# Row tiles in one self attention, activation tables named ahead of use, and the last attention pass kept in PSUM banks

## The chip, the cores and the metric

The kernel runs on one core of one Trainium2 chip. The metric is the device time of one execution in microseconds (us), the median of several runs. One further execution was recorded by the hardware profiler; every duration of a single instruction comes from that one.

## The reference, cut to what matters

Two layers of a Perceiver-like block act on x (128 latents of 256 numbers) with a context of 12544 rows of 192 numbers. All is fp32.

```python
x = x + xattn0(layernorm(x), ctx)   # 16 heads of 16; softmax(q k^T / 4) v over 12544 keys, then relu(o W1 + b1) W2 + b2
x = x + attn0(layernorm(x))         # causal, 16 heads of 16, over the 128 latents, projection
x = x + ffn0(layernorm(x))          # 8 experts 256 -> 1024 -> 256, tanh-gelu, two best experts by a softmax router
x = x + xattn1(layernorm(x), ctx)   # 16 heads of 64; o Wo + bo
x = x + attn1(layernorm(x))         # softmax(x x^T / 16); probabilities under 0.01 are taken out, the others renormalised;
                                    # attended + 0.01 * (sum of those taken out) * (row sums of W)
x = x + ffn1(layernorm(x))          # 8 experts 256 -> 512 -> 256, silu(x G) * (x U) D, two best experts
```

The experts are computed densely: all eight for every latent, weighted by the router (zero for six of them).

## The kernel before, in words

The stages run one after the other, and the names in the trace carry their prefix: x_ in the cross attentions, ln1 to ln5 for the layer norms, k for key tiles made ahead, a_ in the self attentions, f_ in the experts.

**Engines.** TensorE (PE) multiplies into PSUM, eight banks of 128 x 512 fp32. VectorE (DVE), ScalarE (ACT) and GpSimd (POOL) copy, add and exponentiate. SyncE (SP) issues nearly all transfers, in order. Within `tc.manual_schedule()` every engine executes its instructions in the order in which the code writes them; elsewhere a scheduler chooses the order. Before the change, the end of x1 (from the load of Wo), a1 and f1 stand outside it.

**Buffers.** A ring of 28 slots of 128 x 1024 fp32 in SBUF holds score tiles, keys and weights (`slot`, `slot_weight`); a transfer into a slot waits until its last reader is done. In the second half PSUM is split: "s", two tiles of two banks, for scores (`ps_s`, `ps_wide`), and "w", four single banks (`ps_w`, `ps_t`, `ps_mm`). The context is read anew in thirteen superblocks of 1024 rows (the last has 256): `load_context` brings lo (128 rows of features, 512 KB) and hi (64 rows in two halves, 2 x 128 KB).

**x0, to 460 us.** Two octets of eight heads; scores on 32-row tiles of the array (L428: `x_qz`, a copy of q in which the head beside it is zeroed, against `x_kT`); each range of superblocks keeps its own maximum; shift (L506), exponential (L517), attend (L530). Then the ranges are combined (L675 to L703): the negative maxima's least, `fall` = the exponential of the difference, `accs` times `fall`, a sum over the ranges, the division; then W1, W2 and the residual (L706 to L725).

**Key steps.** From there to x1, PE has gaps. `first_keys` (L639 to L660) makes the keys of x1's first pass in 39 steps: for each superblock the 64-row tiles (`tiled`, L209) and two products over 128 rows (`whole`, L212). `fill(n)` makes n steps at the place where it stands. The copies out of the two banks (ACT, L655) are issued when the next superblock is begun. x1's first pass calls fill(2) or fill(1) per period until all are made.

**a0, 481 to 523 us** (L734 to L801). q, k and v are projected; `block_diagonal` (L160) multiplies q with a head mask into a tile of 8 x 128 columns for each eight heads; one matmul per head against the 128 rows of kT gives the scores (L766, a_s); mask, maximum, 16 exponentials (L773), transposition of p in groups of four (a_pT), attend with a column of ones (L785, a_av), division, transposition (a_oT), projection, residual, key steps.

**f0, 523 to 584 us** (L804 to L880). `up` (L824, f_h), bias, gelu (L834), `down` (L841, f_py), each expert's `up` ahead of the former one's `down`. The router (L256 to L300) is a softmax and twice a maximum.

**x1, 584 to 1524 us** (L883 to L1173). Eight passes j of one pair of heads (64 numbers each), thirteen periods s each; a period t makes keys, scores (L958), a copy with the running maximum (ACT L975, DVE L982 of the score tiles, two of 128 x 1024 per period, one for the last superblock), values (L227, L234), and, LAG = 14 periods later, the attend (L1043). At a pass's end the maximum is folded (DVE L1005), transposed (x_mt), negated, spread over the partitions by PE (x_mb) and copied by ACT (x_spread, L1017). The next pass's periods then shift the saved scores by it (`shifted`, L1024: POOL, but DVE in the last pass), exponentiate (L1032), attend; sums of p go by DVE and POOL (L1066, L1071), in the last pass by DVE into one tile (L1062); DVE adds each period's o (L1081). A denominator is the sums against ones (L1089). After the last scores (t = NP = 104) fourteen periods are left that make values and attend: the tail. Then Wo, row bo (L126), residual.

**a1, 1524 to 1541 us** (L1178 to L1222): row sums of W (a_pc, L1182, copied by ACT, L1184), scores, exponential (L1193), a row of small DVE operations, attend, x5. **f1, 1541 to 1588 us** (L1225 to L1261): for each expert gating and up (L1249), silu (L1253), product (f_fuse, L1255), down (L1258), weighted sum.

An ACT function that lies in another table set than the one before is preceded by an ACT_TABLE_LOAD, which the compiler places directly ahead of it: it stands in the trace under the line of that function.

## Time and profile before

| | us |
|---|---|
| median of three runs | 1596.47 |
| the three | 1592.82, 1597.17, 1596.47 |
| the profiled execution: its own time | 1592.66 |
| its span | 1590.9 |

| stage | us from the span's start |
|---|---|
| x0 | 0 to 460 |
| combine, W1, W2, ln1 | 460 to 481 |
| a0 | 481 to 523 |
| f0 | 523 to 584 |
| x1 with its tail (from 1447) | 584 to 1524 |
| a1 | 1524 to 1541 |
| f1, output | 1541 to 1591 |

A timeline line gives start, duration, engine, line, operation, out<-in, sizes, number, and in brackets how long the engine stood idle before it and what released it. Consecutive instructions of a kind are put together. In a line of a stage's busy times, "PEclk" is the mean clock that was granted to TensorE, 1.00 being full.

### The profile page before, as it was taken

To read this page: it belongs to the slowest core of one execution; us is meant where nothing else is said; L and a number is where in the kernel's file an instruction comes from. 1 tells how busy PE (TensorE), PEld (TensorE's weight loads), DVE (VectorE), ACT (ScalarE), POOL (GpSimd) and SP (SyncE) were. 2 spreads that over 40 slices of the span, in tenths; PEclk is the share of its full clock that TensorE was granted. 3 is DMA by queue.
4 is the path that set the end of the run, shared out by engine and by line. 5 is a ranking of instruction groups with operands and counts; after the bars stand their busy time and mean duration, and the time that the engine had idled before them with its cause. 6 is when DMAs were issued, how large, how long until landed. Compare 5 with 4: busy or idle time off the path is not lost.

```text
span 1590.9 us, 39751 instructions
## 1 busy us (share of the span) xinstructions
PE 1507.9 (95%) x17130; PEld 1156.8 (73%) x17130; DVE 1169.4 (74%) x1238; ACT 996.3 (63%) x1221; POOL 851.1 (54%) x559
## 2 busy tenths in 40 slices
PE   7999989999789998999999999999999999999978
PEld 4566666666545877877778787787787777777868
DVE  4798978999863327677777777777777777778952
ACT  5898979889853225665655665565665655655531
POOL 0588877888820000863863864864764764761000
PEclk9999999999997999999999999999999999999979
DMA  3211112111193661322222222232232222225930
GB/s 104 61 41 42 46 42 61 41 42 46 47 270 129 238 167 25 98 84 83 83 80 86 81 81 86 80 93 74 87 94 80 87 81 86 81 81 153 306 135 4
DMA packets 68737, 146.62 MB, mean 92 GB/s; under 512 B 8905, under 2 KB 27089, under 8 KB 68562
## 3 DMA queue, kind: packets, MB, share of 16 engines
q1 hardware_dynamic: 68258, 143.30, 30.0%
q8 instruction: 135, 2.21, 0.6%
q10 hardware_dynamic: 304, 0.79, 0.2%
q14 instruction: 40, 0.33, 0.1%
HBM read 143.92 MB, written 0.13 MB: 91 GB/s over the span
## 4 chain that ended last, share of the span: by engine, by line
PE 62%; DVE 6%; ACT 2%; POOL 1%; DMA 1%; issue 1%; SPq 0%; DVEq 0%; ACTq 0%
PE x_s L958 11%; PE x_v L234 10%; PE x_o L1043 10%; PE x_k L212 9%; PE x_v L227 5%; PE x_k L209 4%; PE f_h L1249 2%; PE f_h L824 2%; PE k L212 2%; PE f_py L841 2%; DVE x_part L1066 1%; POOL x_p L506 1%; PE k L209 1%; DVE x_folded L1005 1%; PE f_py L1258 1%
## 5 line engine op out<-in xcount | busy, mean ns | idle before, releaser
L1024 POOL TENSOR_TENSOR x_p<-x_p,x_spread 128x1024 f32<-128x1024 f32 (+1 forms) x175 | 402.6, 2324 | 165.1 <-ACT x_spread L1017 164.9
L506 POOL TENSOR_TENSOR x_p<-x_p,x_spread 128x512 f32<-128x512 f32 (+1 forms) x184 | 325.6, 1820 | 121.0 <-ACT x_spread L494 61.1
L1066 DVE TENSOR_REDUCE x_part<-x_p 128x256 f32<-128x1024 f32 (+1 forms) x175 | 329.4, 1923 | 1.6 <-ACT x_p L1032 1.6
L975 ACT COPY x_p<-x_s 128x1024 f32<-128x1024 f32 (+1 forms) x200 | 198.0, 996 | 177.7 <-DVE x_mx L982 97.9
L982 DVE TENSOR_TENSOR x_mx<-x_s,x_mx 128x1024 f32<-128x1024 f32 (+1 forms) x161 | 193.4, 1201 | 127.1 <-PE x_s L958 118.7
L1071 POOL TENSOR_TENSOR x_sums<-x_sums,x_part 128x256 f32<-128x256 f32 x161 | 118.7, 738 | 303.4 <-DVE x_part L1066 303.1
L441 ACT COPY x_p<-x_s 128x1024 f32<-128x1024 f32 x196 | 193.4, 1016 | 48.5 <-PE x_s L428 33.2
L234 PEld LDWEIGHTS x_v<-ywv_lo,x_ctx_lo 128*128 128x128 f32 x1568 | 189.3, 192 | 38.3 <-issue 36.8
L1032 ACT ACTIVATE x_p<-x_p 128x1024 f32<-128x1024 f32 (+1 forms) x200 | 197.8, 1037 | 1.4 <-DVE x_p L1024 1.3
L517 ACT ACTIVATE x_p<-x_p 128x1024 f32<-128x1024 f32 x196 | 196.3, 1062 | 0.2 <-DVE x_p L506 0.2
L1043 PE MATMUL x_o<-x_p,x_v 128*64 128x128 f32 x3136 | 193.6, 276 | 0.4
L234 PE MATMUL x_v<-ywv_lo,x_ctx_lo 128*128 128x128 f32 x1568 | 193.1, 276 | 0.0
L447 DVE TENSOR_TENSOR x_mx<-x_s,x_mx 128x1024 f32<-128x1024 f32 x140 | 168.2, 1221 | 32.1 <-PE x_s L428 17.2
L1043 PEld LDWEIGHTS x_o<-x_p,x_v 128*64 128x64 f32 x3136 | 169.6, 137 | 12.3 <-issue 1.5
L958 PE MATMUL x_s<-x_qT,x_kT 64*128 64x128 f32 x2744 | 177.7, 279 | 0.0
L212 PE MATMUL x_k<-x_ctx_lo,ywk_lo 128*128 128x512 f32 (+1 forms) x364 | 171.6, 594 | 0.0
L958 PEld LDWEIGHTS x_s<-x_qT,x_kT 64*128 64x128 f32 x2744 | 160.2, 188 | 15.6 <-issue 15.4
L943 ACT COPY x_v<-x_v 128x512 f32<-128x512 f32 (+1 forms) x208 | 116.2, 563 | 79.3 <-PE x_v L234 78.8
L227 PEld LDWEIGHTS x_v<-ywv_hi,x_ctx_hi 64*128 64x128 f32 x1568 | 106.8, 188 | 48.4 <-issue 25.1
L428 PE MATMUL x_s<-x_qz,x_kT 32*128 32x256 f32 x1568 | 117.6, 401 | 17.7 <-ACT x_p L441 16.6
L530 PE MATMUL x_o<-x_p,x_v 128*32 128x128 f32 x3136 | 111.7, 276 | 10.0 <-ACT x_p L517 8.5
L530 PEld LDWEIGHTS x_o<-x_p,x_v 128*32 128x32 f32 x3136 | 81.9, 109 | 53.9 <-ACT x_p L517 18.9
(257 smaller groups left out, 1761.1 us busy)
## 6 DMA issues: line engine op xcount, KB each, us to landing
x_ctx_lo<-in_ctxT_dram SPq DMA_DIRECT2D x119, 512.0 KB, 4.0
x_ctx_hi<-in_ctxT_dram SPq DMA_DIRECT2D x238, 128.0 KB, 3.8
f_w<-in_L_ffn_W_dram SPq DMA_DIRECT2D x32, 512.0 KB, 4.9
k_lo<-in_ctxT_dram SPq DMA_DIRECT2D x12, 512.0 KB, 10.0
f_gating<-n_kernel_gating_EDF_dram SPq DMA_DIRECT2D x8, 512.0 KB, 6.9
f_up<-L_ffn_kernel_up_EDF_dram SPq DMA_DIRECT2D x8, 512.0 KB, 7.5
f_wd<-ffn_kernel_down_EFD_dram SPq DMA_DIRECT2D x8, 512.0 KB, 7.3
k_hi<-in_ctxT_dram SPq DMA_DIRECT2D x24, 128.0 KB, 7.9
```

The lines of the kernel that those rows point to most:

```text
L212: nc.tensor.matmul(ps[r][:, :h], wk[0][:, js], lo[:, r * h : (r + 1) * h], start=False, stop=True)
L234: nc.tensor.matmul(ps[r][:, kc * P : (kc + 1) * P], lo[:, r * h + kc * P : r * h + (kc + 1) * P], wv[0][:, js], start=False, stop=True, sk ...
L441: nc.scalar.copy(ps[t][k], st[k].rearrange("p a n -> p (a n)"))
L506: engine.tensor_tensor(v, v, by[:, banks].unsqueeze(2).to_broadcast([P, n, 2, 256]), ALU.add)
L517: nc.scalar.activation(ps[t][k], ps[t][k], AF.Exp)
L530: nc.tensor.matmul(os[b][32 * i : 32 * i + 32, u * P : (u + 1) * P], v[:, 2 * g + c, 17 * (2 * i + u) : 17 * (2 * i + u) + 32], p[i // 2][ ...
L958: nc.tensor.matmul(st[:, u, c * P : (c + 1) * P], kTs[t][rs, ks], qT[rs, j, :], start=True, stop=True)
L975: nc.scalar.copy(scores_kept(ps[t][i], sts[i].shape[2] // P), sts[i])
L1024: engine.tensor_tensor(v, v, spreads[j].unsqueeze(2).to_broadcast([P, 2, n, P]), ALU.add)
L1032: nc.scalar.activation(v, v, AF.Exp)
L1043: nc.tensor.matmul(o[us, 0:P], vs[t][:, c0 + c, us], p[:, n0 : n0 + P], start=(c0 + c == 0), stop=(c0 + c == total - 1), skip_group_check= ...
L1066: nc.vector.tensor_reduce(part, v, AX.X, ALU.add)
```

## The change

- `table(func, name)` is a one-column ACTIVATE whose result nobody reads: it makes the table set load where it stands. Exp after each layer norm's std; Sqrt ahead of ln1 to ln5; Gelu in f0's router; Silu in f1.
- x0's two octets are combined each by itself (`octet`), the first one inside x0, after the last shift.
- Key banks are copied right after each `whole`, and the steps are spread anew: 7 instead of 11 in the combine, 15 instead of 13 in a0 with what follows up to x2, 26 instead of 28 in all before x1.
- a0's scores: q is kept in two copies (heads of one parity each), and each of 16 matmuls uses a 32-row tile of the array; scores and p lie in another order of heads.
- x1's last pass: when the last scores are read, their two double banks become `sums` (DVE adds p there) and `both` (PE accumulates o over all periods in one bank; the other takes the projection by Wo and the row sums of W). The shift of the first tile of a period stays on DVE and reads the spread in PSUM, that of the second goes to POOL. Wo is loaded at t = NP+1, seven of the projection's eight matmuls stand at t = NP+3. The contexts of t = NP+2, +5, +8, +11 go to ring slots.
- a1 and f1 are put in a written order; all of f1's weights are issued there, after the last context; expert e+1's gating and up stand ahead of e's down.

The diff, cut to its core:

```diff
@@ -126,6 +126,11 @@
+    def table(func, name):
+        scratch = small.tile([P, 1], F32, tag="table", name=name)
+        nc.scalar.activation(scratch, eps, func)
@@ -133,6 +138,7 @@
+        table(AF.Exp, name + "_table")
@@ -546,6 +550,24 @@
+            def octet(j, out):
+                bs = slice(j * nr, (j + 1) * nr)
+                allneg = small.tile([P, 8], F32, tag="allneg", name=f"x0_allneg{j}", bufs=1)
+                nc.vector.tensor_reduce(allneg, negmax[:, bs].rearrange("p b h -> p h b"), AX.X, ALU.min)
+                fall = small.tile([P, nr, 8], F32, tag="fall", name=f"x0_fall{j}", bufs=1)
+                nc.vector.tensor_tensor(
+                    fall, allneg.unsqueeze(1).to_broadcast([P, nr, 8]), negmax[:, bs], ALU.subtract
+                )
+                nc.scalar.activation(fall, fall, AF.Exp)
+                nc.vector.tensor_tensor(
+                    accs[:, bs], accs[:, bs], fall.unsqueeze(3).to_broadcast([P, nr, 8, 17]), ALU.mult
+                )
+                nc.vector.tensor_reduce(
+                    out.rearrange("p h d -> p (h d)"), accs[:, bs].rearrange("p b h d -> p (h d) b"),
+                    AX.X, ALU.add,
                 )
@@ -606,6 +628,8 @@
+                    if o == len(groups) - 1:
+                        octet(0, acc[0])
@@ -637,25 +661,16 @@
-                    out = None
...
-                        if out:
-                            out()
...
-                        whole(0)
-                        yield
-                        whole(1)
-                        def out(s=s, h=h, pk=pk):
-                            for r in range(2):
-                                nc.scalar.copy(firstk[s][:, r * h : (r + 1) * h], pk[r][:, :h])
-                        yield
-                    out()
+                        for r in range(2):
+                            whole(r)
+                            nc.scalar.copy(firstk[s][:, r * h : (r + 1) * h], pk[r][:, :h])
+                            yield
@@ -667,39 +682,22 @@
...
+                om, o = misc[:, :D], misc[:, D : 2 * D]
+                acc.append(misc[:, 512 : 512 + 8 * 17].rearrange("p (h d) -> p h d", d=17))
+                octet(1, acc[1])
+                table(AF.Sqrt, "ln1_table0")
...
+                    nc.vector.reciprocal(rden, acc[j][:, :, 16])
...
+                        acc[j].rearrange("p (u i) d -> p u i d", u=2)[:, :, :, 0:16],
...
+                fill(3)
@@ -722,7 +720,7 @@
-                fill(3)
+                fill(2)
@@ -737,7 +735,8 @@
-            qbd = work.tile([P, NH, P], F32, tag="qbd", name="a0_qbd")
+            qz = work.tile([P, 2, 2, P], F32, tag="qz", name="a0_qz")
@@ -749,7 +748,8 @@
-                    block_diagonal(work, qT, j, qbd)
+                    for u in range(2):
+                        nc.vector.tensor_scalar(qz[:, j, u, :], qT, parity[:, u : u + 1], None, ALU.mult)
@@ -759,21 +759,34 @@
+            heads = [[8 * g + 2 * (2 * k + i) + u for i in range(2) for g in range(2) for u in range(2)] for k in range(2)]
+            st = [ps_wide(f"a0_s{k}").rearrange("p a (b n) -> p a b n", n=P) for k in range(2)]
+            for g in range(2):
+                for u in range(2):
+                    for i in range(4):
+                        rs = slice(32 * i, 32 * i + 32)
+                        nc.tensor.matmul(
+                            st[i // 2][:, i % 2, 2 * g + u, :], qz[rs, g, u, :], kT[rs, g, :], start=True, stop=True
+                        )
...
+            fill(1)
+            for k in range(2):
+                sm = work.tile([P, 8, P], F32, tag="sm", name=f"a0_sm{k}", bufs=2)
+                nc.vector.tensor_tensor(
+                    sm, st[k].rearrange("p a b n -> p (a b) n"), causal.unsqueeze(1).to_broadcast([P, 8, P]), ALU.add
+                )
+                nmax = small.tile([P, 8], F32, tag="a_nmax", name=f"a0_nmax{k}")
...
+                p = work.tile([P, 8, P], F32, tag="ap", name=f"a0_p{k}", bufs=2)
...
+                if k:
+                    table(AF.Sqrt, "ln2_table0")
+                fill(1)
...
+            fill(2)
@@ -842,7 +856,7 @@
-        best = router(pl[:, :NE], "f0")
+        best = router(pl[:, :NE], "f0", AF.Gelu_apprx_tanh)
@@ -853,6 +867,8 @@
+                if e + 2 == NE:
+                    table(AF.Sqrt, "ln3_table0")
@@ -914,7 +930,9 @@
-            ctxs[t] = load_context(work, f"x1_ctx{t}", (t + 1) % NS, 2)
+            place = slot if t >= NP and (t - NP) % 3 == 2 else None
+            ctxs[t] = load_context(work, f"x1_ctx{t}", (t + 1) % NS, 2, place=place)
@@ -1011,19 +1029,25 @@
+            if j == PASSES - 1:
+                final["sums"] = ps_s("x1_sums")
+                final["both"] = ps_s("x1_both")
...
+            if j == PASSES - 1:
+                final["spread"] = pb
...
-            for p, (c0, n) in zip(ps[t], tiles_of(s)):
+            for i, (p, (c0, n)) in enumerate(zip(ps[t], tiles_of(s))):
...
-                engine = nc.gpsimd if j < PASSES - 1 else nc.vector
-                engine.tensor_tensor(
-                    v, v, spreads[j].unsqueeze(2).to_broadcast([P, 2, n, P]), ALU.add
-                )
+                engine, by = nc.gpsimd, spreads[j]
+                if j == PASSES - 1 and (i == 0 or s == 0):
+                    engine, by = nc.vector, final["spread"][:, : 2 * P].rearrange("p (u q) -> p u q", q=P)
+                engine.tensor_tensor(v, v, by.unsqueeze(2).to_broadcast([P, 2, n, P]), ALU.add)
@@ -1033,7 +1057,8 @@
-            o = ps_w(f"x1_o{t}")
+            whole = j == PASSES - 1
+            o = final["both"][:, 0] if whole else ps_w(f"x1_o{t}")
@@ -1041,8 +1066,9 @@
-                            o[us, 0:P], vs[t][:, c0 + c, us], p[:, n0 : n0 + P], start=(c0 + c == 0),
-                            stop=(c0 + c == total - 1), skip_group_check=True,
+                            o[us, 0:P], vs[t][:, c0 + c, us], p[:, n0 : n0 + P],
+                            start=(c0 + c == 0 and (s == 0 or not whole)),
+                            stop=(c0 + c == total - 1 and (s == NS - 1 or not whole)), skip_group_check=True,
@@ -1054,12 +1080,15 @@
+                total = final["sums"]
+                if s == NS - 1:
+                    return
...
-                    sums[j] = work.tile([P, 2, KB], F32, tag="wide", name=f"x1_sums{t}")
+                    nc.vector.tensor_copy(total, scores_kept(p, n))
...
-                dst = sums[j][:, :, : n * P]
-                old = scores_kept(ps[t][0], 4) if s == 0 else dst
-                nc.vector.tensor_tensor(dst, scores_kept(p, n), old, ALU.add)
+                if (s, i) == (NS - 2, len(tiles) - 1):
+                    sums[j] = work.tile([P, 2, KB], F32, tag="wide", name="x1_allsums")
+                nc.vector.tensor_tensor(sums.get(j, total), scores_kept(p, n), total, ALU.add)
@@ -1074,6 +1103,8 @@
+            if j == PASSES - 1:
+                return
@@ -1083,25 +1114,53 @@
+            parts = [(sums[j], c) for c in range(sums[j].shape[2] // P)]
+            if j == PASSES - 1:
+                n = tiles_of(NS - 1)[0][1]
+                parts += [(scores_kept(ps[NP - 1][0], n), c) for c in range(n)]
+            for i, (part, c) in enumerate(parts):
...
+                        pd[64 * u : 64 * u + 64, 0:P], ones[:, 0:64], part[:, u, c * P : (c + 1) * P],
+                        start=(i == 0), stop=(i == len(parts) - 1), skip_group_check=True,
...
+            if j < PASSES - 1:
+                nc.vector.reciprocal(pd[:, 0:P], pd[:, 0:P])
+                nc.vector.tensor_tensor(oT[:, j, :], os[j], pd[:, 0:P], ALU.mult)
+            else:
+                os[j] = work.tile([P, P], F32, tag="o", name=f"x1_rden{j}", bufs=2)
+                nc.vector.reciprocal(os[j], pd[:, 0:P])
+        def projected(j0, j1):
+            for j in range(j0, j1):
+                nc.tensor.matmul(
+                    final["both"][:, 1, :D], oT[:, j, :], ywo[j // 4][:, j % 4, :], start=(j == 0), stop=False
+                )
...
+                if before == NP - 1:
+                    pass_end(PASSES - 1)
...
+                if t == NP + 1:
+                    context(t)
+                    ywo.extend(
+                        slot_weight(f"ywo{i}", a["L1_xattn_Wo"][512 * i : 512 * i + 512]) for i in range(2)
+                    )
+                if t == NP + 3:
+                    for c in range(2):
+                        nc.tensor.matmul(
+                            final["both"][:, 1, D : 2 * D], ones, awT[:, c, :], start=(c == 0), stop=(c == 1)
+                        )
+                    projected(0, PASSES - 1)
+                if t != NP + 1 and (NS <= t + 1 < NP or 0 <= e + 1 < NP):
@@ -1119,6 +1178,8 @@
+                    if e == NP - 1:
+                        table(AF.Sqrt, "ln4_table0")
@@ -1153,35 +1214,34 @@
+                final_v = v and t == NP - 1
+                if final_v:
+                    for f in v[1:]:
+                        for r in range(2):
+                            f(r)
...
+                if v and not short and not final_v:
...
+            nc.vector.tensor_tensor(oT[:, PASSES - 1, :], final["both"][:, 0, 0:P], os[PASSES - 1], ALU.mult)
+            projected(PASSES - 1, PASSES)
+            py = final["both"][:, 1]
+            add_row(py[:, :D], ROW_BO, D)
+            x = residual(x, py[:, :D], "x4")
+            wsum = final["both"][:, 1, D : 2 * D]
+    with tc.tile_pool(name="l1a", bufs=1) as work, tc.manual_schedule():
...
@@ -1191,6 +1251,7 @@
+        table(AF.Sqrt, "ln5_table0")
@@ -1222,43 +1283,65 @@
+    with tc.tile_pool(name="l1f", bufs=2) as work, tc.manual_schedule():
...
+        gu = [
+            [slot_weight(f"f1_{k}{e}", a[f"L1_ffn_kernel_{k}_EDF"][e]) for k in ("gating", "up")]
+            + [slot_weight(f"f1_wd{e}", a["L1_ffn_kernel_down_EFD"][e])]
+            for e in range(NE)
+        ]
+        def up(e, st, i):
+            for f in range(4):
+                fs = slice(f * P, (f + 1) * P)
+                for c in range(2):
+                    nc.tensor.matmul(
+                        st[:, i, fs], gu[e][i][:, c, fs], xnT[:, c, :], start=(c == 0), stop=(c == 1)
+                    )
+        def gate(e, st):
+            act = work.tile([P, 512], F32, tag="act", name=f"f1_act{e}")
+            nc.scalar.activation(act, st[:, 0, :], AF.Silu)
+            return act
+        def fused(e, st, act):
+            fuse = work.tile([P, 4, P], F32, tag="fuse", name=f"f1_fuse{e}")
+            nc.vector.tensor_tensor(fuse.rearrange("p f n -> p (f n)"), st[:, 1, :], act, ALU.mult)
+            return fuse
+        st = ps_wide("f1_h0")
+        for i in range(2):
+            up(0, st, i)
...
+        table(AF.Silu, "f1_table")
...
+        fuse = fused(0, st, gate(0, st))
...
+            if e + 1 < NE:
+                st = ps_wide(f"f1_h{e + 1}")
+                up(e + 1, st, 0)
+                act = gate(e + 1, st)
+                up(e + 1, st, 1)
+                following = fused(e + 1, st, act)
...
+                nc.tensor.matmul(py[:, :D], fuse[:, f, :], gu[e][2][:, f, :], start=(f == 0), stop=(f == 3))
...
+            fuse = following
```

## The prediction, made before the changed kernel ran

> **What bounds the kernel now.** I read the page's totals, then the busy time of the engines by stage, TensorE's timeline in the first self attention, and the chain that ended last from 1450 us on.
>
> ```profile
> span 1590.9 us, 39751 instructions
> ...
> PE 1507.9 (95%) x17130; PEld 1156.8 (73%) x17130; DVE 1169.4 (74%) x1238; ACT 996.3 (63%) x1221; POOL 851.1 (54%) x559
> ```
>
> TensorE bounds the whole. A gain is possible only where it idles, runs at half clock, or does work that goes. The stages (columns: stretch, its length, busy us of PE, PEld, DVE, ACT, POOL with counts, granted clock, DMA share, GB/s):
>
> ```profile
> 460.00:481.00 21.00, 19.62 (x66) 8.79 (x66) 9.75 (x21) 5.09 (x8) 0.12 (x1) 0.92 1.00 293
> 481.00:525.00 44.00, 40.73 (x154) 24.42 (x154) 14.62 (x24) 15.27 (x32) 0.00 (x0) 0.77 0.36 121
> ...
> 743.50:1447.20 703.70, 698.64 (x7728) 558.99 (x7728) 540.84 (x475) 419.08 (x541) 446.73 (x294) 1.00 0.28 84
> 1447.20:1524.60 77.40, 72.79 (x874) 64.89 (x874) 70.41 (x76) 41.84 (x58) 3.21 (x3) 1.00 0.93 285
> 1524.60:1541.10 16.50, 6.21 (x20) 4.27 (x21) 7.73 (x27) 5.18 (x7) 0.00 (x0) 0.58 0.10 32
> 1541.10:1587.00 45.90, 44.49 (x318) 42.44 (x319) 12.00 (x34) 6.53 (x11) 0.00 (x0) 0.97 0.00 1
> ```
>
> The steady passes (743 to 1447) are 99% PE, and the order of instructions there hardly changes: nothing to win. What is left is the front (460 to 525: combine and self attention a0, clock 0.77), the tail of the last pass (DVE 70.41 and PE 72.79 of 77.4, DMA share 0.93), a1 (a chain, PE idle) and the end of f1.
>
> ```profile
> 485.58 3.84 PE L766 MATMUL a_s<-a_kT,a_qbd 128*128 128x128 f32 x32
> 489.35 1.12 PE L209 MATMUL k<-k_hi,k_wk_hi 64*128 64x512 f32 x2
> 492.97 2.03 PE L209 MATMUL k<-k_hi,k_wk_hi 64*128 64x512 f32 x2 [2.50 <-issue]
> ```
>
> The scores of a0 take 3.84 us; then PE stands still 2.5 us, and the same key tiles cost 2.03 us instead of 1.12: half clock, until 517 but for 500 to 503. Last, pieces of the final chain (start, us, what):
>
> ```profile
> 1457.10 5.14 DMA x_ctx_hi<-in_ctxT_dram
> ...
> 1482.44 4.91 DMA x_ctx_hi<-in_ctxT_dram
> 1487.39 2.35 DVE x_p L1024 x2
> ...
> 1520.31 3.65 PE x_py L1173 x16
> ...
> 1529.04 0.37 ACT a_wsum L1184
> 1529.43 1.28 ACT L1193
> ...
> 1584.29 0.61 ACT f_act L1253
> 1584.92 0.70 DVE f_fuse L1255
> ```
>
> The tail waits for contexts and for DVE's shift, then for the projection; a1 for a copy and an unnamed ACT instruction, which the timeline calls ACT_TABLE_LOAD; f1's end for ACT and DVE.
>
> **What the Trainium skill says.** "ScalarE: Activation LUTs", section What ACT_TABLE_LOAD costs: a change of table set is 1283 ns of load plus about 1380 ns of drain. The trace agrees on the load (1.28 us each) and shows no drain: a_e starts 0.01 us after its load; I use 1.28. "TensorE: Matmul & The Clock Gate", Part 1: half clock after about 3.4 us idle, full again after as long busy. The trace agrees only roughly: 2.5 us of idle sufficed to halve it at 493, and it took 6 us of busy PE to come back. Part 3 of that page: four 32-row tiles run 3.07 times as fast; the trace has such tiles only in L428.
>
> **The change, part by part.** All against the profiled execution, 1592.66 us with its 1590.9 us span.
>
> *Combine.* An octet's correction moves behind the last shift and one is made earlier. DVE does the same multiplications and reductions in two halves; I find the sum o 0.6 us later than 467.0. But four key steps fewer (about 1.0 us each, L209 1.12, L212 0.96) stand between it and ln1's input, some of them in PE time that waits anyway: 1.7 us earlier (474.4 for 476.1).
>
> *a0.* ln1's std waited for the load 477.80 to 479.08: -1.3. Scores on row tiles: L428 makes 1568 passes of 256 columns in 117.6 us, 75 ns each; 32 passes of 128 columns are 1.2 us if the rate halves, 2.4 if not; I take 1.6, so -2.2. The two block-diagonal products (1.23 us each) lie beside PE's projections: nothing. So the scores end at 484.2, not 489.35 (-5.2). Then DVE (2 x 2.45) and 16 exps (4.83) follow to about 491.6. Keys evicted at once put ACT copies of k_3 behind those exps and the preloaded Sqrt table (1.28), and a_p's transposition needs their banks: 493.7 instead of a start at 497.65 to 498.5. Some 3 us of PE idle remain, so I leave the half clock as it is. The same four key steps precede a_oT: 511.05 for 515.10. a0 with the combine: **-4.05** at f0's first matmul; ln2's and Gelu's loads go, but PE was busy with keys and f_h beside them.
>
> *f0 and pass 0.* Before f0's first down product two key steps stand now (1.72 us), then one: **-0.85**. 28 steps are made ahead of x1's loop before, 26 after, so pass 0 gets two more, 1.9 us of PE. PE idles 3.9 of 10 us at 625 to 635 while DVE's maxima (9.25 of 10) finish, so I charge half: **+0.9** (bounds 0 and 1.9). ln3's load (579.67) was hidden already.
>
> *Tail.* From 1461.39 to 1515.26 ten attends took 5.39 us each, while their PE work is 1.09+1.98+1.90 = 4.97. DVE gives up one of two shifts (1.18) to POOL (2.32 in L1024's row, fits in 4.97) and the o additions (0.28); f1's weights leave the DMA queues until all contexts are issued. So PE's rate: 10 x 0.42 = -4.2. The shift reads PSUM, not ACT's copy, and ywo's two loads stand behind context NP+1 in SP's queue, not ahead of it: -1.0 at its start. New on PE: seven projections (0.456 each) and the ones product (0.86) at t=NP+3: +4.0. SP: context NP+2 goes to a slot freed only when DVE has copied the first tile into sums (about 1462.9); with 4.9 us of landing it is there at 1467.3, needed at 1465.7: +1.9 with the restart (bounds 0 and 4), all later contexts and weights behind it in SP's queue. End: 9.36 us from 1515.26 to the residual become 7.1 (one projection of 0.46 for 3.65; four denominators more, 0.55; last additions gone): -2.3. Sum **-1.6** (bounds -3.5 and +0.5).
>
> *a1.* pc, its copy and a_e's table load leave the chain: a_e at 1529.4 for 1530.72, and a_vs (0.17) joins it: **-1.1**.
>
> *f1.* up(0) is moved ahead of the router, the gate of e+1 before py(e), so the last f_act and f_fuse hide behind py(6): **-1.4** (1584.27 to 1585.67). The weights: 24 x 512 KB from about 1500 at 308 GB/s (1.7 us each) have landed at 1541; expert 7 wants its at 1575. Cover 30 us; without it each us late costs one.
>
> *Start.* Each preload is a load of 1.28 and a tiny ACTIVATE (13 more ACT instructions in all, about 0.2 us each, in ACT's idle time but for the Sqrt in a0 named above). Exp's load moves to 6.7 us, where ACT idles until 11.18; 1.28 leaves ACT at t=13, not a bound there: 0.
>
> Sum: -4.05-0.85+0.9-1.6-1.1-1.4 = **-8.1**. The profiled time is at the low end of the runs shown (1592.82, 1597.17, 1596.47), which fall in two groups; the middle of all four, 1594.6, is my base: 1594.6 - 8.1 = **1586.5 us**. About 0.3% (4.8 us) is what a measurement of this kernel can tell from no change.
>
> **Rivals.** *The half clock goes too* (full 12%): if the shorter gap keeps PE warm, of the 8 us that 493 to 517 lose (k 2.03 for 1.12, 3.78 for 1.98), 5 come back: -13, 1581.5. Against it: idle time remains, and a_av at 507.84 ran at half clock with no gap ahead of it.
>
> *Absorbed* (22%): a0's gain dies at f0, whose weights still arrive at the old times (DMA share 0.61 there, 1.00 at 460 to 481), and pass 0 pays its two steps in full. Then only tail, a1 and f1 count: -1.6-1.1-1.4+0.6 = -3.5, 1591.1.
>
> *Contexts tied to score slots* (slower, 5%): contexts NP+2, +5, +8, +11 each wait for a slot of a score tile. If each is issued when PE already wants it, each costs its landing of 4.9 us: 19.6, of which 1.9 is counted: -8.1+17.7 = +9.6, 1604.2. The change breaks even at 2.5 us a context ((8.1+1.9)/4) and is slower beyond 0.3% from 3.7. For it: 5.14 and 4.91 on the chain; against: three contexts ahead instead of two.
>
> *Nothing reaches the end* (3%): 1594.6.
>
> **From these to the numbers.** Forecast 58%. Faster: nearly all of the forecast (0.55), the warm clock (0.12), half of the absorbed case (0.11): 0.78. Same: 0.17. Slower: 0.05. Range: below, the warm clock with no context stall (1579.5); above, the absorbed case with the tail's upper bound (1593.2).
>
> **What would show it.** Right: a_s near 1.6 us at 482 to 484; f0's first f_h near 521; attends 5.0 us apart in the tail; x4's residual near 1519.0 (1524.62 less 4.0 of the front and 1.6 of the tail); no gap before py(7). Wrong: PEclk 1.00 at 493 to 517; gaps before f_h with DMA as releaser; gaps at x_v of the last pass above 2 us; POOL late before x_p's exps. The prediction fails most likely in a0, where its largest term rests on a queue of banks that the trace of before does not show.

## The result and the profile after

| | before | after |
|---|---|---|
| median of six runs each, us | 1596.01 | 1603.46 |
| their range | 1592.17 to 1598.1 | 1600.25 to 1604.62 |
| the profiled execution: own time, span | 1592.66, 1590.9 | 1604.62, 1602.9 |

The changed kernel is slower: ratio 1.0046, 95% interval 1.0028 to 1.0064. The forecast was 1586.5 us, 8.1 us less than before; what came is 7.5 us more. The page's totals of the kernel after:

```profile
span 1602.9 us, 39793 instructions
...
PE 1512.1 (94%) x17138; PEld 1162.0 (72%) x17138; DVE 1154.9 (72%) x1219; ACT 997.8 (62%) x1234; POOL 873.5 (54%) x570
```

TensorE (PE) has 4.2 us more busy time, and 7.8 us more in which it stands still. To find where, I cut both traces at the same marks: x0's last copied maximum (L498 after, x_spread), the std of each layer norm, the first f_h, the spreads of x1's passes, the output's transfer. Differences are after minus before; the forecast's terms are beside them.

| stage, from mark to mark | before, us | after, us | change | forecast |
|---|---|---|---|---|
| x0, to its last spread | 439.55 | 443.73 | +4.18 | 0 |
| combine, W1, W2, to ln1's std | 39.55 | 39.38 | -0.17 | -3.0 |
| a0, ln1's std to f0's first f_h | 45.91 | 44.19 | -1.72 | -1.05 |
| f0, to ln3's std | 60.37 | 59.51 | -0.86 | -0.85 |
| x1's beginning, ln3's std to the second spread | 168.00 | 177.10 | +9.10 | +0.9 |
| from there to ln4's std | 772.38 | 769.60 | -2.78 | -1.6 |
| a1, ln4's std to ln5's | 11.99 | 11.19 | -0.80 | -1.1 |
| f1, ln5's std to the output | 50.46 | 55.51 | +5.05 | -1.4 |
| sum | | | +12.00 | -8.1 |

(The forecast's -4.05 for the front is split here into combine and a0, as its text gives ln1's std: 1.7 and 1.3.)

Three rows ask for a cause: x1's beginning, f1, and the combine that didn't shorten. The x0 row is chance. PE executes the same instructions in the same order there, but in the profile of before its clock became full at about 12 us (x_early's matmuls take 0.71 us), after at about 20.5 us (the same ones take 1.22). In the eleven profiles other than before's, x0's first spread lies between 58.5 and 60.9 us, also at 60.27 in E5 below, whose start is exactly that of before; before's 57.03 was a lucky one. So of the 12.0 us between these two profiles 4.2 are not the change's, which leaves 7.8, near the 7.5 of the medians.

Now the stages of the kernel after, busy times and columns as in the prediction (length, busy us of PE, PEld, DVE, ACT, POOL, clock, DMA share, GB/s). In order: ln1's std to f0, f0's end with x1's beginning, the tail, f1:

```profile
484.00:527.30 43.30, 39.43 (x162) 23.78 (x162) 13.76 (x28) 15.81 (x36) 0.00 (x0) 0.76 0.43 126
585.60:753.00 167.40, 155.52 (x1695) 121.98 (x1696) 114.03 (x102) 97.00 (x122) 72.20 (x46) 0.99 0.29 76
1456.00:1532.40 76.40, 74.17 (x904) 65.99 (x901) 57.27 (x54) 42.69 (x61) 27.74 (x14) 1.00 0.68 215
1548.00:1600.00 52.00, 46.85 (x321) 43.52 (x320) 12.57 (x35) 6.73 (x12) 0.00 (x0) 0.95 0.03 9
```

a0 still runs at 0.76 of the clock (before 0.77). In x1's beginning PE is idle 12 us of 167, in f1 5 of 52, at full clock or nearly so: these are waits. In the tail the change does what was forecast: DVE has 57.27 us of work where it had 70.41, and DMA share falls from 0.93 to 0.68.

**The wait in f1.** PE's timeline of one expert, after (start, duration, engine, line, operation, and in brackets the idle time before it and its releaser):

```profile
1560.26 1.95 PE L1301 MATMUL f_h<-ln5T,f_gating 128*128 128x128 f32 x16
1562.90 2.05 PE L1301 MATMUL f_h<-ln5T,f_up 128*128 128x128 f32 x16 [0.69 <-ACT f_act L1307]
1564.79 1.89 PE L1340 MATMUL f_py<-f_wd,f_fuse 128*128 128x256 f32 x8
```

The up product waits for f_act, ACT's silu, which reads the gating product, though it needs nothing that the silu makes. Both products lie in the two banks of one tile of `ps_wide`; the change writes the silu (`gate`) between the two `up` calls, so the write of the second bank is ordered behind the read of the first. The expert takes 6.25 us. Before, it was 5.41 us from one up product to the next, with no wait ahead of it:

```profile
1555.23 1.95 PE L1249 MATMUL f_h<-ln5T,f_up 128*128 128x128 f32 x16
1560.64 1.95 PE L1249 MATMUL f_h<-ln5T,f_up 128*128 128x128 f32 x16
```

Seven times 0.84 us are 5.9.

**The wait in x1's beginning.** PE of the kernel before, whose scores (x_s) come without a wait here:

```profile
592.79 2.06 PE L958 MATMUL x_s<-x_qT,k 64*128 64x128 f32 x32
```

PE and ACT of the kernel after, the same stretch:

```profile
605.80 2.08 PE L976 MATMUL x_s<-x_qT,k 64*128 64x128 f32 x32 [1.59 <-ACT x_p L993]
607.81 1.12 PE L212 MATMUL k<-k_lo,k_wk_lo 128*128 128x512 f32 x2
608.86 1.13 PE L209 MATMUL k<-k_hi,k_wk_hi 64*128 64x512 f32 x4
```

```profile
604.25 0.58 ACT L672 COPY k<-k 128x512 f32<-128x512 f32 x1 [3.17 <-PE k L212]
604.73 1.94 ACT L993 COPY x_p<-x_s 128x1024 f32<-128x1024 f32 x2
```

ACT stands still 3.17 us for a key product (L212) while finished scores lie in PSUM: the key's copy, issued as soon as its product is (`fill`), stands ahead of the period's score copies (`keep`) in ACT's queue, but PE makes the product after the scores. Then PE waits 1.59 us for a score bank. My theory for this row is that order in ACT's queue; the rival is the forecast's own term, two more key steps for PE in x1, at its upper bound and with late score banks on top.

**The combine.** DVE's timeline, after:

```profile
465.00 0.42 DVE L544 COPY x_oT<-x_o 128x256 f32<-128x256 f32 x1 [4.91 <-PE x_o L534]
466.09 0.87 DVE L565 TENSOR_TENSOR x_accs<-x_accs,x_fall 128x680 f32<-128x680 f32 x1
466.99 1.36 DVE L568 TENSOR_REDUCE x_acc<-x_accs 128x136 f32<-128x680 f32 x1
468.26 0.29 DVE L550 COPY x_accs<-x_ot 128x136 f32<-128x136 f32 x1
```

DVE is idle 4.91 us, and then the first octet's correction (0.87 and 1.36) stands ahead of the copy (468.26) for which the last octet's waits. Before, that copy stood directly behind the one before it:

```profile
460.03 0.43 DVE L540 COPY x_oT<-x_o 128x256 f32<-128x256 f32 x1 [3.97 <-PE x_o L530]
460.99 0.30 DVE L546 COPY x_accs<-x_ot 128x136 f32<-128x136 f32 x1 [0.53 <-PE x_ot L245]
```

PE stops with DVE, and comes back at half clock (L209 takes 2.08 us here for the four that take 1.13 above):

```profile
468.60 1.22 PE L126 MATMUL bvb_ps<-rows,ones 1*128 1x256 f32 x2 [2.69 <-DVE x_accs L550]
469.75 2.08 PE L209 MATMUL k<-k_hi,k_wk_hi 64*128 64x512 f32 x4
```

So the theory: A, f1's ordering by tile; B, ACT's queue in x1's beginning; C, the place of octet(0). Each was undone alone, by moving lines only.

### The profile page after: what moved, and what is told of

Same layout as the page of the kernel before. It is cut to its first block, busy times and chain, and to the rows that moved or that the text cites. A ratio compares the mean times of both kernels' runs of the same rounds, so it can differ in the third digit from the quotient of the medians.

```text
span 1602.9 us, 39793 instructions
## 1 busy us (share of the span) xinstructions
PE 1512.1 (94%) x17138; PEld 1162.0 (72%) x17138; DVE 1154.9 (72%) x1219; ACT 997.8 (62%) x1234; POOL 873.5 (54%) x570
## 4 chain that ended last, share of the span: by engine, by line
PE 65%; DVE 7%; ACT 4%; issue 1%; POOL 1%; DMA 1%; SPq 0%; DVEq 0%; ACTq 0%
PE x_v L234 11%; PE x_s L976 11%; PE x_o L1068 9%; PE x_k L212 9%; PE x_v L227 5%; PE x_k L209 4%; PE f_h L1301 2%; PE f_h L838 2%; PE f_py L855 2%; PE k L212 1%; DVE x_part L1095 1%; PE x_both L1068 1%; POOL x_p L510 1%; PE f_py L1340 1%; DVE x_mx L451 1%
## 5 line engine op out<-in xcount | busy, mean ns | idle before, releaser
L1050 POOL TENSOR_TENSOR x_p<-x_p,x_spread 128x1024 f32<-128x1024 f32 (+1 forms) x186 | 427.5, 2325 | 169.4 <-ACT x_spread L1041 169.1
L212 PE MATMUL x_k<-x_ctx_lo,ywk_lo 128*128 128x512 f32 (+1 forms) x364 | 171.6, 594 | 0.0
L1068 PE MATMUL x_o<-x_p,x_v 128*64 128x128 f32 x2744 | 169.6, 276 | 0.4
L1068 PEld LDWEIGHTS x_o<-x_p,x_v 128*64 128x64 f32 x2744 | 148.4, 137 | 11.0 <-issue 1.7
```

The lines of the kernel that those rows point to most:

```text
L212: nc.tensor.matmul(ps[r][:, :h], wk[0][:, js], lo[:, r * h : (r + 1) * h], start=False, stop=True)
L1050: engine.tensor_tensor(v, v, by.unsqueeze(2).to_broadcast([P, 2, n, P]), ALU.add)
L1068: nc.tensor.matmul(o[us, 0:P], vs[t][:, c0 + c, us], p[:, n0 : n0 + P], start=(c0 + c == 0 and (s == 0 or not whole)), stop=(c0 + c == tot ...
```

## The experiments

Edits are shown against the changed kernel unless said otherwise; each ratio is against the kernel before.

**E1, f1's gate behind both up products.**

```diff
-                up(e + 1, st, 0)
-                act = gate(e + 1, st)
-                up(e + 1, st, 1)
-                following = fused(e + 1, st, act)
+                for i in range(2):
+                    up(e + 1, st, i)
+                following = fused(e + 1, st, gate(e + 1, st))
```

> The changed kernel with one edit: in the second experts, silu's read of expert e+1's gating bank is written behind both of its products (gating and up), not between them. My theory: the first up product of each expert waits for ACT's read of the other bank of the same two-bank tile (0.66 us of f_act and about 0.2 of restart, seven times): PE's period per expert falls from 6.25 to about 5.41 us and the whole by 5.9 us, to about 1597.5 against 1603.5. Rival: the experts wait for their weights, which are all issued behind the last context: then the wait only changes its name to a DMA and the time stays within 1 us of 1603.5.

Measured: 1.0014 (1.0007 to 1.0022). f1 takes 48.83 us for 55.51, an expert 5.30 for 6.25. PE in E1:

```profile
1563.49 1.95 PE L1301 MATMUL f_h<-ln5T,f_gating 128*128 128x128 f32 x16
1565.27 1.95 PE L1301 MATMUL f_h<-ln5T,f_up 128*128 128x128 f32 x16
```

The bracket is gone, with the same work and the silu issued later. A holds, and f1 is then 1.63 us shorter than before: the forecast's -1.4 was there, under the wait.

**E2, the key steps behind the period's score copies.**

```diff
-                if t < NS:
-                    fill(2 if t < 4 else 1)
...
                     keep(t, sts, evicted if short else None)
+                if t < NS:
+                    fill(2 if t < 4 else 1)
```

> The changed kernel with one edit: in the first pass of the second cross attention, the key steps are written behind the period's score copies instead of ahead of them, so that in ACT's queue the score copies no longer stand behind the copy of a key bank, which waits for a product that PE makes after the scores. Number and size of all instructions are the same. My theory: the idle gaps of PE before the scores (1.59 us, four times, and smaller ones) go; the first pass ends 8 to 9 us earlier; 1603.5 falls to about 1595. Rival: the pass is later because it holds two more key steps (1.9 us of PE) and ends on DVE's maxima: then this edit changes less than 1 us.

Measured: 1.0002 (0.9991 to 1.0012). x1's beginning takes 168.04 us, for 177.10 with the change and 168.00 before. PE makes the same instructions as in the kernel after, in the same order but for two key products that change places with query projections; what differs is ACT's queue. PE, then ACT:

```profile
601.69 2.06 PE L976 MATMUL x_s<-x_qT,k 64*128 64x128 f32 x32
603.67 1.13 PE L212 MATMUL k<-k_lo,k_wk_lo 128*128 128x512 f32 x2
604.73 1.13 PE L209 MATMUL k<-k_hi,k_wk_hi 64*128 64x512 f32 x4
605.69 1.95 PE L976 MATMUL x_s<-x_qT,k 64*128 64x128 f32 x32
```

```profile
602.90 1.93 ACT L993 COPY x_p<-x_s 128x1024 f32<-128x1024 f32 x2 [0.52 <-PE x_s L976]
604.84 0.59 ACT L672 COPY k<-k 128x512 f32<-128x512 f32 x1
```

The scores are copied first, the key's copy finds its product done, and no wait is left on PE. B holds. The rival falls: the two extra steps are still in E2, and cost nothing that the stage shows. Of the 9.1 us 7.5 are waits ahead of the transposition of the pass's maximum (x_mt), which starts 56.99 us behind ln3's std in the kernel after, 49.53 in E2 and 49.48 before. The other 1.6 are half clock behind it. That half clock isn't tied to these waits: E4 and E6 to E10, all with this edit, take 169.64 to 169.70 us, 1.6 more than E2.

**E3, octet(0) two groups earlier**, where DVE was idle.

```diff
+                    if o == len(groups) - 3:
+                        octet(0, acc[0])
                     if o is not None:
...
-                    if o == len(groups) - 1:
-                        octet(0, acc[0])
```

> The changed kernel with one edit: the first octet's combination is written two groups earlier, so that on DVE it stands directly behind the last shift and ahead of the copy of the last attended tile. My theory: it stood ahead of the copy of the turned tile, 2.3 us on the path, while DVE had been idle 4.9 us before: the combine ends about 2.3 us earlier, less 0.25 us for an exponential that now stands between the last groups' exponentials on ACT: 1603.5 falls to about 1601.5. Rival: PE's key steps and their banks set the end of the combine anyway: no change (within 0.5 us) at the first layer norm behind it.

Measured: 0.9995 (0.9982 to 1.0008), the runs spread from 1588.9 to 1602.1. From x0's last spread to ln1's std it takes 33.96 us for 39.38. DVE in E3:

```profile
461.54 0.87 DVE L565 TENSOR_TENSOR x_accs<-x_accs,x_fall 128x680 f32<-128x680 f32 x1 [0.59 <-ACT x_fall L564]
462.44 1.39 DVE L568 TENSOR_REDUCE x_acc<-x_accs 128x136 f32<-128x680 f32 x1
...
464.57 0.42 DVE L544 COPY x_oT<-x_o 128x256 f32<-128x256 f32 x1 [0.63 <-PE x_o L534]
465.52 0.30 DVE L550 COPY x_accs<-x_ot 128x136 f32<-128x136 f32 x1 [0.53 <-PE x_ot L245]
```

The correction fills the idle time; counted from x0's last spread, the copy stands 3.0 us earlier (21.57 us behind it for 24.53). That is the direct part. The rest of the 5.4 us is clock: the ones product and the eight key products behind it take 0.69, 1.13 and 1.98 us in E3, where they took 1.22, 2.08 and 3.30. C holds, for the 3.0 us. That the gap brought the half clock isn't shown: in E7 and E9, with the octet early as here, PE waits 0.53 and 0.39 us right ahead of these products, and yet four of the key products take 3.53 and 3.57 us for 1.98. Their combine takes 35.55 and 35.34 us, for 33.95 to 33.97 in E4, E8 and E10. So C is worth from 3 to 5.4 us, as the clock falls out. The wide range of the runs may come from the clock in a0, seen next; one profile can't tell.

**E4, all three edits.** [The three diffs above together.]

> The changed kernel with the three edits together (gate after up, key steps after the score copies, octet two groups earlier). My theory: 5.9 + 8.5 + 2.1 = 16.5 us less than the changed kernel, about 1587 against 1596 of the kernel before: what remains is the sum of the gains of a0, tail, a1 and f1's end that I had forecast (about -8 to -10). Rival: the three waits hide behind one another or behind late weights: no better than 1596.

Measured: 0.9903 (0.9887 to 0.9918), 1577.41 us. The three single gains against the changed kernel's 1.0046 are 0.32, 0.44 and 0.51 points, 1.27 together; E4 is 1.43 below it, 26 us where 16.5 were expected. The surplus isn't one of the three. From the profile of after to that of E4 it is 27.0 us: 5.4 in the combine, 7.5 in x1's beginning and 6.6 in f1 are 19.5, but 7.2 lie in a0, which none of the edits touches. The three causes do account for the loss and for a gain behind it. In a0 E3 and E4, the same program up to x1, differ too. Lines from ln1's std to ln2's, E3 and E4:

```profile
477.91:516.09 38.18, 33.96 (x148) 20.86 (x144) 13.30 (x26) 13.32 (x33) 0.00 (x0) 0.78 0.57 161
```

```profile
477.83:509.53 31.70, 27.48 (x148) 16.24 (x144) 13.21 (x26) 13.31 (x32) 0.00 (x0) 0.95 0.61 170
```

6.5 us apart, with the same work, at another clock (0.78 and 0.95). In both, PE stands 2.99 us for ACT's copy of k before a_pT; half clock then lasts about 17 us in one and 3.4 in the other. E8 takes this up.

**E5, the other direction: the kernel before, with its keys evicted at once.** Nothing else of the change; against the kernel before:

```diff
-                        def out(s=s, h=h, pk=pk):
-                            for r in range(2):
-                                nc.scalar.copy(firstk[s][:, r * h : (r + 1) * h], pk[r][:, :h])
-                        yield
-                    out()
+                        for r in range(2):
+                            whole(r)
+                            nc.scalar.copy(firstk[s][:, r * h : (r + 1) * h], pk[r][:, :h])
+                            yield
```

> The kernel before with one part of the change alone: the copies of a key bank are issued right behind its product, the spread of the key steps stays as it was. My theory: in the first pass of the second cross attention the score copies then stand behind key copies that wait for later products, and the pass gets 5 to 8 us longer, with PE idle ahead of the scores until ACT's score copies: about 1600 against 1594 to 1596. Rival: the loss in that pass of the changed kernel came from the two more key steps: no change (within 1 us) between the third layer norm and the first spread of that attention. Also seen here, as a second look at the start of a kernel without the early table load: if PE's clock warms up late because of that load, the first spread of the first cross attention stays at 57 us; if it is chance, it can be 60 to 61 here too.

Measured: 1.003 (1.0014 to 1.0045). x1's beginning: 178.99 us, 11.0 more than before, so the loss of B comes with this edit alone. PE in E5:

```profile
595.79 2.08 PE L949 MATMUL x_s<-x_qT,k 64*128 64x128 f32 x32 [1.59 <-ACT x_p L966]
```

The same 1.59 as above. What I had not expected: in this profile ln1's std to ln2's takes 28.54 us where before took 42.63, with the old block-diagonal scores; the transpositions of p follow the keys without a gap, at a clock of 0.94. The same edit is good in a0 and bad in x1, and the sum is a loss.

**E6, E4 without the preloads of tables** (`table()` left empty).

```diff
-        scratch = small.tile([P, 1], F32, tag="table", name=name)
-        nc.scalar.activation(scratch, eps, func)
+        return
```

> The kernel with the three edits, and table() emptied, so that every table set is loaded where its function first needs it, as before the change. My theory: the loads come back to the path ahead of the first layer norm behind the combine (1.3 us), ahead of the exponential of the last self attention (1.1 us), and little elsewhere (beside keys and products on PE): 2 to 3 us more than the kernel with the three edits (0.9903 of before), about 0.992. Rival: all the loads lie beside other work or count with a drain [...]: no difference, or 5 us and more.

Measured: 0.9975 (0.9962 to 0.9989); the preloads are worth 0.72 points of E4, about 11 us, of which some 5 lie in a0 (36.96 us at a clock of 0.77, for 31.70), and that is for the most part the clock's chance. The rest is: ln1 2.7 us later (1.28 are the load ahead of its std; the other 1.4 are half clock in key products, as E7 and E9 have it with the preloads), ln2's std to ln3's 69.65 us for 64.76, a1 12.48 for 10.82. The experts f0 were a surprise. ACT and PE in E6:

```profile
529.70 0.58 ACT L671 COPY k<-k 128x512 f32<-128x512 f32 x1 [6.70 <-PE k L211]
530.30 1.28 ACT L847 ACT_TABLE_LOAD   x1
531.60 2.00 ACT L847 ACTIVATE f_hT<-f_hb 128x1024 f32<-128x1024 f32 x2
```

```profile
532.71 5.41 PE L854 MATMUL f_py<-f_w,f_hT 128*128 128x256 f32 x16 [2.93 <-ACT f_hT L847]
```

The load stands between a key's copy and the first gelu; PE waits 2.93 us, and then runs at half clock, 5.41 us for 3.62 in E4. In E4 the first gelu stands ahead of this copy in ACT's queue (520.25 and 523.20), here behind it. So of the stage's 4.9 us only 1.28 are the load itself; the place in the queue and the clock came with it, and no run has them apart.

**E7, E4 with block-diagonal scores in a0** (whole-array products against the 128 rows of kT, as before the change; `block_diagonal` and `qbd` back in place of `qz`).

```diff
-                            st[i // 2][:, i % 2, 2 * g + u, :], qz[rs, g, u, :], kT[rs, g, :], start=True, stop=True
+                            st[i // 2][:, i % 2, 2 * g + u, :], qbd[:, 8 * g + 2 * i + u, :], kT[:, g, :],
+                            start=True, stop=True,
```

> The kernel with the three edits, and the scores of the first self attention made again from block-diagonal queries on the whole array, in the new order of heads. My theory: the scores take 3.8 us instead of 1.5 and the exponentials start that much later: 2.3 us more up to the second layer norm at equal clock. Rival: the self attention waits for key banks and the clock, not for its scores: within 0.7 us at the second layer norm. Chance in the granted clock there can move either by about 6 us, so the duration of the stage is read at equal clock.

Measured: 0.9908 (0.9894 to 0.9923). By the profiles at equal clock (0.95 both) ln1's std to ln2's is 34.26 us for 31.70: row tiles are worth 2.6 us. The intervals of the two ratios overlap, so the ratios alone couldn't tell it; the stage does.

**E8, E4 with a0's two key copies on DVE.** They stand between the maxima and the gap of 2.99 us; ACT is still in its 16 exponentials there.

```diff
+                            (nc.vector.tensor_copy if on_dve else nc.scalar.copy)(
+                                firstk[s][:, r * h : (r + 1) * h], pk[r][:, :h]
+                            )
...
+                    on_dve.append(1)
                 fill(1)
...
             fill(2)
+            on_dve.clear()
```

> The kernel with the three edits, and the copies of the two key banks made behind the maxima of the first self attention moved from ACT to DVE, which is idle there; ACT's queue then holds only the exponentials and the table load. My theory: the transposition of p no longer waits for banks that ACT empties behind 16 exponentials and the preloaded table (2.99 us of PE idle with ACT as releaser in the changed kernel): PE's idle goes down by 2 to 4 us and the stage with it, if the clock is the same; about 0.988 of before. Rival: p itself is late (the first eight exponentials) and PE waits as long for that: within 0.7 us.

Measured: **0.9857 (0.9841 to 0.9874), 1572.21 us**, the fastest of all. PE after the scores, for E8 and for the kernel after:

```profile
488.61 1.12 PE L209 MATMUL k<-k_hi,k_wk_hi 64*128 64x512 f32 x2 [0.49 <-DVE k L674]
489.66 1.09 PE L155 MATMUL a_pT_ps<-ident,a_p 128*128 128x128 f32 x8
```

```profile
495.95 1.09 PE L209 MATMUL k<-k_hi,k_wk_hi 64*128 64x512 f32 x2 [0.27 <-issue]
500.04 1.97 PE L155 MATMUL a_pT_ps<-ident,a_p 128*128 128x128 f32 x8 [2.99 <-ACT k L672]
```

Without the gap there is no half clock: the eight transpositions take 1.09 us, not 1.97 (1.63 in E4). The stage ln1's std to ln2's in E8:

```profile
475.54:502.83 27.29, 25.84 (x148) 15.20 (x144) 14.33 (x28) 12.25 (x31) 0.00 (x0) 1.00 0.63 193
```

It is 27.28 and 27.29 us in the next two as well, while it was 31.70 to 38.93 in the kernels with the gap and preloads. So the gap made the loss, and very likely the spread of this stage from profile to profile; whether the wide range of E3's runs comes from it too isn't shown.

**E9, E8 with both shifts of the tail on DVE**, to see what the move of one to POOL is worth.

```diff
-                if j == PASSES - 1 and (i == 0 or s == 0):
+                if j == PASSES - 1:
```

> The kernel with the three edits and the two key copies on DVE (0.9857 of before), with one part of the change undone in the last pass's tail: both tiles of a period are shifted by DVE again, none by POOL. My theory: DVE's two shifts and two additions (2 x 1.18 + 2 x 1.23 = 4.8 us) still fit under PE's 4.97 us per period, if barely; what slowed the tail before was the DMA load of the second experts' weights and the o additions with it. So 0 to 2 us more. Rival: DVE was the tail's bound: with 4.8 us plus waits per period the tail goes back to about 5.4 us a period, 4 to 5 us more.

Measured: 0.9887 (0.9858 to 0.9916); from the last spread to ln4's std 72.16 us for 68.39. But not as either theory had it. The periods stay 4.97 us, though DVE works 27.43 of 30 us, so DVE's load of 9.1 tenths does not set them. The loss is at the beginning of the tail. PE in E9:

```profile
1454.74 0.46 PE L227 MATMUL x_v<-ywv_hi,x_ctx_hi 64*128 64x128 f32 x2 [1.85 <-DMA x_ctx_hi<-in_ctxT_dram]
...
1456.52 3.33 PE L234 MATMUL x_v<-ywv_lo,x_ctx_lo 128*128 128x128 f32 x16
```

Context NP+2 is issued by SP's queue 6.5 and 10.0 us behind the last spread in E9 (lo and hi: 1448.49 and 1452.00), in E8 5.4 and 7.8 us behind it (1444.18 and 1446.56). DVE with both shifts comes later to copying the first tile into the sums, so the slot comes free later. PE waits, and then has half clock (3.33 us for 2.05). This is the ring-slot wait that the forecast gave the change at +1.9; it decides only when DVE has both shifts. Whether DVE at 9.8 tenths or a DMA share of 1.0 made the periods of 5.39 before stays open: no run has the one without the other.

**E10, E8 with gating and up in a tile of one bank each, and the gate between them again** (the order that the change writes).

```diff
-                st = ps_wide(f"f1_h{e + 1}")
-                for i in range(2):
-                    up(e + 1, st, i)
-                following = fused(e + 1, st, gate(e + 1, st))
+                st = [ps_mm(f"f1_{k}{e + 1}") for k in "gu"]
+                up(e + 1, st, 0)
+                act = gate(e + 1, st)
+                up(e + 1, st, 1)
+                following = fused(e + 1, st, act)
```

> The kernel with the three edits and the two key copies on DVE (0.9857 of before), in which the second experts' gating and up products have a bank-sized tile each, and silu's read is written between them again, as the change wanted it. My theory: the 0.84 us per expert was a wait for a read of the same two-bank tile, which the recording layer orders as a whole though the read and the write touch different banks; with two tiles there is no such wait: within 0.7 us of the kernel it starts from. Rival: the order of writing alone makes PE wait for ACT, or the four single banks run short: 4 to 6 us more, with ACT as releaser of the up products.

Measured: 0.9864 (0.984 to 0.9889); f1 48.95 us, 5.30 an expert. PE in E10:

```profile
1544.34 1.95 PE L1307 MATMUL f_g<-ln5T,f_gating 128*128 128x128 f32 x16
1546.13 1.95 PE L1307 MATMUL f_u<-ln5T,f_up 128*128 128x128 f32 x16
```

No wait, with the order of A kept. So it was not the order, but the order on one shared tile. Nor does the earlier silu gain anything over E1's.

## Why the prediction was wrong, step by step

**f1, "up(0) is moved ahead of the router, the gate of e+1 before py(e) ... -1.4": the step that fails.** The gain is real (E1: -1.63), but the step looked at what the moved gate releases, not at what is ordered behind it: a matmul into the same two-bank tile. Against E1 it cost 0.95 us an expert, 6.7 us (55.51 for 48.83), and E10 has no such cost with a tile for each bank. The table says +5.05 for -1.4.

**x1's beginning, "28 steps are made ahead of x1's loop before, 26 after ... I charge half: +0.9": the step that fails.** It counted PE's two products and not the ACT copies that the same steps now issue. What is counted cost nothing visible (E2: 168.04 for 168.00); what isn't cost 9.1 us (E2), of which 7.5 are the waits and 1.6 half clock. In E5 it cost 11.0 with the old spread of the steps, so it is where all the copies stand, not the two more. The forecast had followed the same copies through ACT's queue in a0; it did not ask where they stand in the other places that call `fill`.

**Combine, "I find the sum o 0.6 us later ... 1.7 us earlier ... -1.3": the step that fails.** DVE's arithmetic is the same, but octet(0) stands between the last tile's two copies; the forecast read the moved work as work, not as a place in DVE's queue. From x0's last spread the sum o is there 28.53 us later in the kernel after, 27.06 before: 1.5 us late for 0.6. And the four key steps fewer, which were to save 2.3 us between o and the residual, save 0.2 (9.31 us for 9.53), as PE makes the rest at half clock. In E3 o is there after 25.22 us and the residual 7.21 later, so without the wait, and at full clock, the 2.3 are there. The row is -0.17 for -3.0; E3 gains 5.4. The -1.3 for ln1's load is right: E6 has 1.28 us of load ahead of ln1's std.

**a0: right in its parts.** The scores take 1.58 us (489.02 to 490.60) for the 1.6 taken. From their end to the first transposition the forecast had 9.5 us (484.2 to 493.7), the trace has 9.4 (490.60 to 500.04), and the copy of k behind the preloaded table is what ends it. "Some 3 us of PE idle remain, so I leave the half clock": 2.99, 0.76. The stage is -1.72 for -1.05; E7 puts 2.6 us on row tiles. The rival "half clock goes too" came true not with this change but with E8. The closing sentence, that the forecast fails most likely in a0, was wrong: the term it doubted was the one it had worked out.

**f0** -0.86 for -0.85. Of its preloaded table the forecast said that "PE was busy with keys and f_h beside them". In E6, behind the other edits, PE does wait there (2.93 us), though in part for its place in ACT's queue.

**Tail.** Periods of 4.97 us, as forecast; the seven projections and the ones product take 4.1 us (1481.36 to 1485.45) for 4.0. The slot wait of +1.9 is absent (it appears in E9), and the sum is -2.78 for -1.6. That it is so near is in part luck: 1.8 of it lie ahead of the last spread, where PE waits 0.55 us for the folded maximum instead of 2.49, which no term had. Behind the spread it is 68.31 us for 69.30, -1.0: the start is 0.55 us later where 1.0 was to be gained, the periods give 3.35 for 4.2, the end gives the 2.3. The forecast also added its times wrongly here: 1462.9 + 4.9 is 1467.8, not 1467.3. The slower rival, contexts tied to score slots, named this place; it is not where the time went.

**a1** -0.80 for -1.1: a_e starts 4.2 us after ln4's std, for 5.0 before. **Start**, 0: the 4.2 us in the table are chance, as said.

With the start set aside, four of the seven rows came within 1.2 us, and three missed by 2.8, 8.2 and 6.5 us, all in one direction and for one kind of reason: something moved stands ahead of work that another engine waits for, in a queue twice, at a tile once. None of the rivals named one of them. (In the absorbed rival "its two steps in full" would be +1.9 by the forecast's own bound, not the +0.6 of its sum: -2.2 and 1592.4 us. The median lies above that too.)

## What to carry to other kernels

For each instruction that an edit moves, write down what stands behind it in its own engine's queue and whether its input is made before or after theirs: a copy placed "at once" is late for everyone if its product comes later than theirs. Look also at which tile it touches, since a reader of one bank holds back a writer of the other. And when several edits are measured together, undo each alone: here the change as a whole was 0.5% slower, and moving some ten lines of it made it 1% faster than before, with two copies on another engine 1.4%.

## What the runs showed of the hardware

- The length of half clock is not fixed by the gap. Behind the same 2.99 us on the same instructions it lasted about 20 us (after), 17 (E3) and 3.4 (E4). "TensorE: Matmul & The Clock Gate" of the Trainium skill, Part 1, has some 3.4 us of idle before the clock halves and as long busy before it returns: E4 agrees on the return, the others don't: from 500 to 519 us of the kernel after PE is busy 18.96 us of 19.00 at a granted clock of 0.50. At the start the same stream was at full clock after 12 or after 20.5 us.
- Nor does the gap say whether half clock comes. Behind waits of 2.69 us (combine) and 2.99 (a0) it was there. In x1's first pass the same wait of 3.66 us stands ahead of the same products in before and in E5, and these take 1.95 us in one and 3.25 in the other; in E2 they take 1.95 behind 3.30. In E9 the four key products of the combine take 3.57 us for 1.98 with no wait over 0.54 us in the 13 us before them. Before, then E5:

```profile
634.86 0.44 PE L245 MATMUL x_mt<-ident,x_folded 128*128 128x128 f32 x2 [3.66 <-DVE x_kT L931]
635.13 1.95 PE L234 MATMUL x_v<-ywv_lo,x_ctx_lo 128*128 128x128 f32 x16
```

```profile
637.01 0.44 PE L245 MATMUL x_mt<-ident,x_folded 128*128 128x128 f32 x2 [3.66 <-DVE x_kT L922]
637.28 3.25 PE L234 MATMUL x_v<-ywv_lo,x_ctx_lo 128*128 128x128 f32 x16
```

- Where half clock does follow a gap, it can cost as much as the gap: 2.8 us on the products behind 2.69 us of wait in the combine (after against E3), and in E6 1.8 us on the one next group of products behind 2.93.
- "ScalarE: Activation LUTs" of the Trainium skill, section What ACT_TABLE_LOAD costs, adds a drain to the load; here the next ACTIVATE starts 0.02 us after the load's 1.28 (E6, 531.60). Yet f0 is 4.9 us longer without the preloads, with the new order in ACT's queue, the PE wait and the clock behind it.
- Four 32-row tiles at 128 columns run 2.4 times as fast as the whole array with zeroed heads (3.84 to 1.58 us for 32 products).
